# Softmax exponentials turned by a trip through DRAM and VectorE, in place of TensorE transposes

## The chip, the cores and the metric

The kernel runs on one core of one Trainium2 chip. The metric is device time in microseconds (us) of one execution of the whole program; lower is better. The kernel before has a median of 1646.08 us over three runs (1644.12 to 1647.88).

A core has five engines with a queue of instructions each, and each engine takes its own in order: TensorE (PE: matrix products, results to PSUM banks), VectorE (DVE), ScalarE (ACT), GpSimd (POOL) and SyncE (SP, which here only issues DMAs). PEld is the loading of TensorE's stationary operand. DMAs are issued from SP's queue and, a few, from ACT's.

## The reference, cut to what matters

One transformer block on x of 2048 tokens by 1024 channels, all in float32. There is one attention head of width 256.

```
qkv  = layernorm(x) @ Wqkv + bqkv            # 1024 -> 3 x 256
p    = softmax(q @ k.T / 16)                 # 2048 x 2048
attn = (p @ v) @ Wo + bo                     # 256 -> 1024
x1   = x + layernorm(attn)
h    = layernorm(x1)
y    = (silu(h @ Wg.T) * (h @ Wu.T)) @ Wd.T  # 1024 -> 2752 -> 1024
out  = x1 + layernorm(y)
```

## The kernel before, in words

**Precision.** TensorE multiplies in fp32r. Each float32 operand is split into a high part (an ACT copy that rounds) and a low part (VectorE: source minus high part), and a product is three matmuls: high by high, high by low, low by high (`mm3`, lines 126 to 130).

**Stages.** First q, k and v for all tokens (0 to about 140 us of the profiled span). Then attention over 16 blocks of 128 queries (`for i in range(NT)`, to about 410 us). Then the gated feed-forward in two halves of the tokens (the rest, lines 869, 1055 and 1056).

**One attention block i.** The loop body works on three blocks at once:

- `scores(i+1, j)`, j = 0 to 3: six matmuls of 512 columns into `bank[j]`, then a VectorE maximum of the bank (line 265).
- `softmax(i+1)`: two small VectorE operations make the bias (lines 440, 441), ACT takes four exponentials of 512 columns from the banks into `p_s` and sums them (line 443).
- `turn(i, j)`: four TensorE transposes of 128 by 128 from `p_s` into bank 4 or 7 (line 452), then ACT and VectorE split the bank into high and low parts of `pT` (lines 111, 112). It brings keys onto partitions.
- `attend(i)`: 16 pairs of matmuls into `bank[6]`, 512 columns with the high part of p (line 468) and 256 columns with the low part (line 469); ACT copies half of the bank to `o`, VectorE adds the other half (lines 470, 471).
- `turn_o(i-1)`: two TensorE transposes of `o` into `bank[5]` (line 478), split by ACT (480) and VectorE (481) into `oTs`.
- `proj(i-1)`: twelve matmuls of 512 columns of `oTs` by the output weights, into banks 5 and 7; VectorE scales by the softmax denominator and adds the bias (line 491).
- For the first eight blocks (`EARLY`), also: statistics of proj's result (`out_stats`), normalize and add x (`residual`), store x1, normalize again, store the result spread over partitions (`spread`, an ACT-issued DMA, line 597), load it back (`gather`, 600), turn it in 32 by 32 tiles on VectorE (`xpose`, 604), store it (606).

**What sets the order.** The code is given in program order to a planner that holds a cost for each instruction and lays down one fixed order for each engine. `pin` (`tc.keep_in_program_order`) keeps an instruction in the order of the code among others so marked; `tc.issue_after(x)` puts instructions behind x. On the chip each engine follows its fixed order and waits for operands. In the order laid down for the kernel before, TensorE has `turn_o(i-1)`, then `attend(i)`, with `proj(i-1)` and `scores(i+2)` mixed into the latter half, and the transposes of `turn` in groups of four all through the block.

Of the kernel before, what the change touches and what calls it, by code (L numbers as in the profile page):

```python
# [15 lines left out]
P = 128  # L16
# [18 lines left out]
def block_kernel(ctx, tc, x, xt, wqk, wqk_t, wv, bqk, bv, wo, bo, wgu, wlast, wd, out):  # L35
# [48 lines left out]
    x1_d = [tl(dram, [P, C], F32, f"x1_d{t}") for t in range(NT)]  # L84
    xn_d = [tl(dram, [P, C], F32, f"xn_d{t}") for t in range(NT)]
# [172 lines left out]
    def scores(i, j, pin=lambda i: i):  # L258

        cols = slice((i % TB) * P, (i % TB + 1) * P)  # L260
        q = qa if i < TB else qs[(i // TB) % 2]
        for d in range(2):
            k = kT(d, j)
            mm3(bank[j], (q[:, d, 0, cols], q[:, d, 1, cols]), (k[:, 0, :], k[:, 1, :]), d == 0, d == 1, pin)
        nc.vector.tensor_reduce(ys[i % 4][:, j : j + 1], bank[j], AX.X, ALU.max)
# [170 lines left out]

    def softmax(i):

        s = ys[i % 4]
        nc.vector.tensor_reduce(s[:, 4:5], s[:, 0:4], AX.X, ALU.max)  # L440
        nc.vector.tensor_scalar(s[:, 5:6], s[:, 4:5], -1.0 / 16.0, None, ALU.mult)
        for j in range(4):
            nc.scalar.activation(p_s[:, j * 512 : j * 512 + 512], bank[j], AF.Exp, bias=s[:, 5:6], scale=1.0 / 16.0, accum_out=s[:, 8 + j : 9 + j])
        nc.vector.tensor_reduce(s[:, 12:13], s[:, 8:12], AX.X, ALU.add)
        nc.vector.reciprocal(s[:, 13:14], s[:, 12:13])
# [10 lines left out]
    def attend(i):  # L456
# [10 lines left out]
        for k in range(NKB):  # L467
            nc.tensor.matmul(b, p[:, k, 0, :], vt(k).rearrange("p h d -> p (h d)"), start=(k == 0), stop=False)  # L468
            nc.tensor.matmul(b[:, D:], p[:, k, 1, :], vt(k, 0), start=False, stop=(k == NKB - 1))  # L469
# [5 lines left out]
    def turn_o(i, pin=lambda i: i):  # L475
# [4 lines left out]
        last_o[0] = nc.scalar.copy(oTs[i % 2][:, :, 0, :], b)  # L480
        last_o[1] = pin(nc.vector.tensor_tensor(oTs[i % 2][:, :, 1, :], b, f32(oTs[i % 2][:, :, 0, :]), ALU.subtract))
        return t

    def proj(i):
        a = pair[i % 3][0] if i < EARLY else f4[i % 2] if i < NT - 1 else xe
        oT = oTs[i % 2]
        for h, b in ((1, bank[5]), (0, bank[7])):
# [3 lines left out]
            nc.vector.scalar_tensor_tensor(a[:, cols], b, ys[i % 4][:, 13:14], bo_s[:, cols], ALU.mult, ALU.add)  # L491
# [3 lines left out]

    def out_stats(t, a):

        m, r, s = norm_stats([a[:, 0:512], a[:, 512:1024]], tc.keep_in_program_order if t >= EARLY else None)
        nc.gpsimd.tensor_scalar(s[:, 16:17], m, r, -1.0, ALU.mult, ALU.mult)
        return r, s  # L500

    def residual(t, a, xt, st=None, pin=lambda i: i):

        r, s = st or out_stats(t, a)
        pin(nc.scalar.activation(a, a, AF.Identity, bias=s[:, 16:17], scale=r))
        (nc.gpsimd if t >= EARLY else nc.vector).tensor_tensor(xt, xt, a, ALU.add)
# [82 lines left out]

    def wo_split(d):  # L590
        pin(nc.scalar.copy(wo_s[:, d, 0, :], wr[d]))
        pin(nc.vector.tensor_tensor(wo_s[:, d, 1, :], wr[d], f32(wo_s[:, d, 0, :]), ALU.subtract))


    def spread(t, a):

        nc.scalar.dma_start(xn_d[t].rearrange("(i s) (g c) -> i s g c", i=4, g=4).rearrange("i s g c -> (s g) i c"), a.rearrange("p (i c) -> p i c", i=4))
# [605 lines left out]
    room = [(f4[2], f4[3]), (wr[1], xe)]  # L1203
    sts = {}
    for i in range(NT):
# [5 lines left out]
        turn(i, 0)  # L1211
        turn(i, 1)
        if i == NT - 1:
            for f in order[:2]:
                f.use()
            for f, r in zip(order[4:6], f4[2:4]):
                f.load(r)
        if more:
            scores(i + 1, 0)
            scores(i + 1, 1)  # L1220
        turn(i, 2)
        turn(i, 3)
        if more:
            scores(i + 1, 2)
            scores(i + 1, 3)
# [175 lines left out]
```

## Time and profile before

| | |
|---|---|
| median of 3 runs | 1646.08 us (1644.12 to 1647.88) |
| the profiled execution, its own time | 1644.92 us |
| its span in the trace | 1643.1 us |
| PE busy | 1633.6 us (99%) |
| DVE busy | 1122.5 us (68%) |
| ACT busy | 718.2 us (44%) |
| granted TensorE clock, mean | 1.00 |

The span is the time from the first to the last record in the trace; 1.8 us of the execution lie around it. A busy PE is not PE at its peak, since matmuls are pipelined and each lasts longer than the distance to the next. Of use here are therefore the starts: a 512-column matmul follows its predecessor by about 0.23 us, while each record is 0.39 us long. The same holds on a smaller scale for VectorE and ACT, where an operation may start some 0.08 us ahead of the end of the one before it.

### The profile page before, as it was taken

How to read it: one execution, taken by the hardware profiler on the slowest of the kernel's cores; microseconds unless marked ns; L12 is line 12 of the kernel's file. 1: busy time of each engine (PE TensorE's matmuls, PEld its weight loads, DVE VectorE, ACT ScalarE, POOL GpSimd, SP SyncE). 2: the span in 40 equal slices, each digit the busy share in tenths (PEclk: the TensorE clock that was granted, in tenths of full speed). 3: DMA queues.
4: the chain of work that ended last, by engine and by line, in shares of the span. 5: the costliest groups of instructions: out<-in, count | busy, mean ns of one | idle time of the engine just before them, and what ended most of it. 6: DMA issues, size and time to landing. Idle time of an engine off the chain costs nothing.

```text
span 1643.1 us, 20860 instructions
## 1 busy us (share of the span) xinstructions
PE 1633.6 (99%) x7576; PEld 1361.1 (83%) x7576; DVE 1122.5 (68%) x1676; ACT 718.2 (44%) x1061; POOL 108.7 (7%) x157
## 2 busy tenths in 40 slices
PE   9999999999999999999999999999999999999998
PEld 8888888888888888888888888888888888888887
DVE  6656787778778888787577458855666655455458
ACT  5663445436444444433465344433333333354342
POOL 3120000000011111120000001100000000000001
PEclk9999999999999999999999999999999999999999
DMA  9452145556657777677477657532222333686663
GB/s 324 164 178 69 52 158 189 167 199 210 232 172 242 252 252 246 227 237 264 156 250 248 195 182 236 199 104 96 97 96 96 103 103 121 242 260 195 192 190 121
DMA packets 148184, 300.38 MB, mean 183 GB/s; under 512 B 14576, under 2 KB 39792, under 8 KB 148080
## 3 DMA queue, kind: packets, MB, share of 16 engines
q1 hardware_dynamic: 138480, 288.69, 53.1%
q10 hardware_dynamic: 9600, 10.36, 2.0%
q8 instruction: 59, 0.97, 0.2%
q14 instruction: 45, 0.37, 0.1%
HBM read 206.70 MB, written 92.29 MB: 182 GB/s over the span
## 4 chain that ended last, share of the span: by engine, by line
PE 94%; DVE 2%; DMA 2%; issue 1%; ACT 0%; POOL 0%; SPq 0%; POOLq 0%; DVEq 0%; ACTq 0%
PE bank L869 71%; PE bank L128 4%; PE bank L130 4%; PE bank L129 4%; PE bank L468 3%; PE bank L469 2%; PE bank L452 2%; PE bank L246 1%; PE bank L247 1%; PE bank L311 1%; DVE a L112 0%; DMA f<-xn_d 0%; DMA f<-wv 0%; DMA xn_d<-f 0%; PE bank L1056 0%
## 5 line engine op out<-in xcount | busy, mean ns | idle before, releaser
L869 PE MATMUL bank<-a 128*128 128x512 f32 (+1 forms) x960 | 226.4, 386 | 0.0
L869 PE MATMUL bank<-xb,a 128*128 128x512 f32 x912 | 212.5, 389 | 0.1
L869 PEld LDWEIGHTS bank<-a 128*128 128x128 f32 x960 | 179.1, 188 | 36.6
L869 PEld LDWEIGHTS bank<-xb,a 128*128 128x128 f32 x912 | 170.9, 188 | 35.8 <-DVE a L112 0.5
L111 ACT CAST a<-f2p 128x1024 fp32r<-128x1024 f32 (+2 forms) x123 | 106.9, 869 | 124.7 <-PE bank L869 89.5
L112 DVE TENSOR_TENSOR a<-f2p,a 128x1024 fp32r<-128x1024 f32 (+2 forms) x123 | 122.4, 995 | 44.1 <-ACT a L111 37.7
L869 PE MATMUL bank<-kx,a 128*128 128x512 f32 x612 | 145.2, 389 | 0.0
L869 PEld LDWEIGHTS bank<-kx,a 128*128 128x128 f32 x612 | 114.9, 188 | 23.8
L112 DVE TENSOR_TENSOR a<-f,a 128x1024 fp32r<-128x1024 f32 (+1 forms) x70 | 79.9, 1141 | 61.3 <-ACT a L111 59.0
L869 PE MATMUL bank<-wvo 128*128 128x512 f32 (+1 forms) x498 | 120.9, 387 | 0.0
L869 PEld LDWEIGHTS bank<-wvo 128*128 128x128 f32 x498 | 93.0, 188 | 18.9
L111 ACT CAST a<-f 128x1024 fp32r<-128x1024 f32 (+1 forms) x70 | 57.6, 823 | 101.1 <-PE bank L869 96.2
L869 PE MATMUL bank<-a,a 128*128 128x512 f32 x420 | 99.6, 389 | 0.3 <-ACT p_s L931 0.3
L869 PE MATMUL bank<-kx,wvo 128*128 128x512 f32 x420 | 99.3, 389 | 0.0
L883 DVE TENSOR_TENSOR xi<-bank,xi 128x512 f32<-128x512 f32 (+1 forms) x90 | 60.9, 681 | 48.5 <-PE bank L869 42.2
L869 PEld LDWEIGHTS bank<-a,a 128*128 128x128 f32 x420 | 78.8, 188 | 17.1 <-ACT p_s L931 0.8
L869 PEld LDWEIGHTS bank<-kx,wvo 128*128 128x128 f32 x420 | 78.8, 188 | 16.3
L112 DVE TENSOR_TENSOR wvo<-f,wvo 128x1024 fp32r<-128x1024 f32 (+1 forms) x47 | 54.6, 1162 | 53.1 <-ACT wvo L111 53.1
L869 PE MATMUL bank<-a1b,wvo 128*128 128x512 f32 x360 | 86.6, 389 | 0.0
L883 DVE TENSOR_TENSOR p_s<-bank,p_s 128x512 f32<-128x512 f32 x80 | 53.9, 681 | 46.7 <-PE bank L869 42.9
L869 PEld LDWEIGHTS bank<-a1b,wvo 128*128 128x128 f32 x360 | 67.6, 188 | 14.0
L869 PE MATMUL bank<-kx 128*128 128x512 f32 (+1 forms) x339 | 78.5, 387 | 0.0
(341 smaller groups left out, 3063.7 us busy)
## 6 DMA issues: line engine op xcount, KB each, us to landing
f2p<-wgu SPq DMA_DIRECT2D x41, 512.0 KB, 5.5
f<-x SPq DMA_DIRECT2D x28, 512.0 KB, 6.0
f<-wgu SPq DMA_DIRECT2D x22, 512.0 KB, 3.5
wr<-wgu SPq DMA_DIRECT2D x21, 512.0 KB, 4.9
hd_S<-xi SPq DMA_DIRECT2D x42, 256.0 KB, 4.4
f<-wd SPq DMA_DIRECT2D x20, 512.0 KB, 4.1
td_T<-f SPq DMA_DIRECT2D x40, 256.0 KB, 5.0
f2p<-td_T SPq DMA_DIRECT2D x40, 256.0 KB, 3.0
```

Of the source, the lines that this page charges most:

```text
L111: nc.scalar.copy(hi, src)
L112: (lo_engine or nc.vector).tensor_tensor(lo, src, f32(hi), ALU.subtract)
L128: pin(nc.tensor.matmul(o, w[0], m[0], start=first, stop=False))
L129: pin(nc.tensor.matmul(o, w[0], m[1], start=False, stop=False))
L130: return pin(nc.tensor.matmul(o, w[1], m[0], start=False, stop=last))
L246: pin(nc.tensor.matmul(b, xg[:, c, 0, cols], wv_s[:, c, :, :].rearrange("p a f -> p (a f)"), start=(c == 0), stop=False))
L247: pin(nc.tensor.matmul(b[:, D:], xg[:, c, 1, cols], wv_s[:, c, 0, :], start=False, stop=(c == 7)))
L452: nc.tensor.transpose(b[:, n * P : (n + 1) * P], p_s[:, k * P : (k + 1) * P], ident)
L468: nc.tensor.matmul(b, p[:, k, 0, :], vt(k).rearrange("p h d -> p (h d)"), start=(k == 0), stop=False)
L469: nc.tensor.matmul(b[:, D:], p[:, k, 1, :], vt(k, 0), start=False, stop=(k == NKB - 1))
L869: one = nc.tensor.matmul(o, w[i], m[j], start=first and n == 0, stop=last and n == 2, skip_group_check=chained)
L883: nc.vector.tensor_tensor(o, a, b, op)
```

## The change

For query blocks 2 to 12 (`SPREAD`) the TensorE transposes of p go away. ACT writes the exponentials into `p_s` in another order within a partition, and after each half (two banks) issues a DMA that stores 512 KB into `pt_d`, spread so that its 1 KB pieces change partitions (`by_quarter`). In the next block SP loads each half back (`collect`) into `wr[0]` and `wr[1]`, VectorE turns it there in 32 by 32 tiles (`turn_half`, 1024 columns), ACT takes the high part (`high_half`) and VectorE the low part (`low_half`), again 1024 columns each.

The queries of a block come out permuted, which `turn_o` undoes with a strided read of the bank. The steps of such a block are pinned on VectorE and ACT in the order of the code, and `attend(i)` is put behind `proj(i-1)` on TensorE, with its matmuls grouped by eight: eight of 512 columns, then eight of 256.

The early norms are computed otherwise. The rows of the output weights and the bias are centred (`minus_mean`, `wo_split`, `center_bo`: ACT sums, POOL scales, ACT subtracts), so that proj's result has mean zero and its scale needs only ACT's sum of squares (`out_stats`). The residual is one VectorE operation (a * r + x), and the second norm uses the mean of x and ACT's sum of squares. VectorE's four `bn_stats` of a block go; ACT gets two squares in place of one scaling. `first_sums` uses other tiles (`room`).

```diff
+    SPREAD = range(2, NT - 3)
+    def by_quarter(d):
+        return d.rearrange("(i s) (g c) -> i s g c", i=4, g=4).rearrange("i s g c -> (s g) i c")
+    def collect(i):
+        for h in range(2):
+            nc.sync.dma_start(wr[h], pt_d[i][h])
+    def turn_half(i, h):
+        pin(nc.vector.transpose(wr[h], wr[h]))
+    def high_half(i, h):
+        high, low, r = half_of(i, h)
+        pin(nc.scalar.copy(high, r))
+    def low_half(i, h):
+        high, low, r = half_of(i, h)
+        pin(nc.vector.tensor_tensor(low, r, f32(high), ALU.subtract))
...
+            pin(nc.scalar.activation(o, b, AF.Exp, bias=s[:, 5:6], scale=1.0 / 16.0, accum_out=s[:, 8 + j : 9 + j]))
+            if i in SPREAD and j % 2 == 1:
+                pin(nc.scalar.dma_start(by_quarter(pt_d[i][h]), p_s[:, h * C : h * C + C].rearrange("p (i c) -> p i c", i=4)))
...
-        for k in range(NKB):
-            nc.tensor.matmul(b, p[:, k, 0, :], vt(k).rearrange("p h d -> p (h d)"), start=(k == 0), stop=False)
-            nc.tensor.matmul(b[:, D:], p[:, k, 1, :], vt(k, 0), start=False, stop=(k == NKB - 1))
+        n = 8 if i in SPREAD else 1
+        for k0 in range(0, NKB, n):
+            for k in range(k0, k0 + n):
+                nc.tensor.matmul(b, p[:, k, 0, :], vt(k).rearrange("p h d -> p (h d)"), start=(k == 0), stop=False)
+            for k in range(k0, k0 + n):
+                nc.tensor.matmul(b[:, D:], p[:, k, 1, :], vt(k, 0), start=False, stop=(k == NKB - 1))
...
     def out_stats(t, a):
-        m, r, s = norm_stats([a[:, 0:512], a[:, 512:1024]], tc.keep_in_program_order if t >= EARLY else None)
-        nc.gpsimd.tensor_scalar(s[:, 16:17], m, r, -1.0, ALU.mult, ALU.mult)
-        return r, s
+        s = small_tile()
+        nc.scalar.activation(xe, a, AF.Square, accum_out=s[:, 0:1])
+        return scale_of(s)
+    def residual(t, a, xt, r, pin):
+        pin(nc.vector.scalar_tensor_tensor(xt, a, r, xt, ALU.mult, ALU.add))
+        nc.sync.dma_start(x1_d[t].rearrange("(g s) c -> s g c", g=4), xt)
+        s, m = small_tile(), m_of(t // TB, t % TB)
+        nc.gpsimd.tensor_scalar(s[:, 4:5], m, -1.0, None, ALU.mult)
+        nc.scalar.activation(a, xt, AF.Square, bias=s[:, 4:5], accum_out=s[:, 0:1])
+        r = scale_of(s)
+        nc.gpsimd.tensor_tensor(s[:, 5:6], s[:, 4:5], r, ALU.mult)
+        nc.scalar.activation(a, xt, AF.Identity, bias=s[:, 5:6], scale=r)
...
     for i in range(NT):
+        if i in SPREAD:
+            collect(i)
+            scores(i + 1, 0, hold=pin)
+            scores(i + 1, 1, hold=pin)
+            turn_half(i, 0)
+            high_half(i, 0)
+            scores(i + 1, 2, hold=pin)
+            scores(i + 1, 3, hold=pin)
+            largest(i + 1, pin)
+            turn_o(i - 1, hold=pin)
+            turn_half(i, 1)
+            exponentials(i + 1, (0, 1), pin)
+            high_half(i, 1)
+            exponentials(i + 1, (2, 3), pin)
+            low_half(i, 0)
+            projected = proj(i - 1, pin)
+            low_half(i, 1)
+            denominator(i + 1, pin)
...
+        if i in SPREAD:
+            with tc.issue_after(projected.ins):
+                attend(i)
```

The order that the planner lays down for the changed program, from block 4 on, is for TensorE: the last 13 of the 24 matmuls of `scores(i+1)` (banks 1 to 3), the two transposes of `turn_o(i-1)`, the twelve of `proj(i-1)` (two into bank 7, six into bank 5, four into bank 7), eight of `attend(i)` with 512 columns, eleven of `scores(i+2)` (banks 0 and 1), eight of 256, eight of 512 and eight of 256 columns, which ends `attend(i)`. For VectorE: the addition that ends `attend(i-1)`, the maxima of banks 0 and 1, `turn_half(i, 0)`, the maxima of banks 2 and 3, `largest`, the low part of `turn_o(i-1)`, `turn_half(i, 1)`, `low_half(i, 0)`, the two scalings of `proj(i-1)`, `low_half(i, 1)`, `denominator`, `residual(i-2)`, `xpose(i-3)`. For ACT: the copy that ends `attend(i-1)`, `high_half(i, 0)`, the high part of `turn_o(i-1)`, two exponentials, a DMA issue, `high_half(i, 1)`, two exponentials, a square, a DMA issue, a square, a scaling, a DMA issue.

## The prediction

> **What bounds the kernel now.** I read the page's busy table and its list of waits for TensorE first, to see which engine sets the time and whether it ever starves. Then the chain that ended last, for the length of one attention block, and the timeline of one block's end, for the steps that the change puts between products.
>
> ```profile
> PE 1633.6 (99%) x7576; PEld 1361.1 (83%) x7576; DVE 1122.5 (68%) x1676; ACT 718.2 (44%) x1061; POOL 108.7 (7%) x157
> ...
> PE bank L128 <- DVE oTs L481: 0.8, 2, 0.4
> ```
>
> TensorE is busy all through, and in the whole run it waits 0.8 us for `oTs`, the operand of `proj`. So only fewer or shorter TensorE steps gain, and any new wait of TensorE costs its full length.
>
> ```profile
> 263.36 0.44 PE bank L452 x4
> ...
> 343.01 0.44 PE bank L452 x4
> ...
> 273.73 0.27 PE L469 MATMUL bank<-a1b,a 128*128 128x256 f32 x1
> 273.84 0.40 PE L128 MATMUL bank<-wvo,oTs 128*128 128x512 f32 x1
> 274.04 0.37 ACT L470 COPY f<-bank 128x256 f32<-128x256 f32 x1 [1.03 <-PE bank L469]
> 274.45 0.42 DVE L471 TENSOR_TENSOR f<-bank,f 128x256 f32<-128x256 f32 x1
> ...
> 228.39 1.24 DVE L604 STREAM_TRANSPOSE f<-f 128x1024 f32<-128x1024 f32 x1
> 229.55 0.11 DVE L122 TENSOR_SCALAR small<-small 128x1 f32<-128x1 f32 x1
> 229.58 0.68 DVE L265 TENSOR_REDUCE ys<-bank 128x1 f32<-128x512 f32 x1
> 230.18 0.68 DVE L118 BATCH_NORM_STATS2 small<-f 128x6 f32<-128x512 f32 x1
> 230.77 0.68 DVE L265 TENSOR_REDUCE ys<-bank 128x1 f32<-128x512 f32 x1
> 231.36 0.41 DVE L481 TENSOR_TENSOR oTs<-bank,oTs 128x256 fp32r<-128x256 f32 x1
> ...
> 187.47 1.05 ACT L434 CAST qb<-f 128x1024 fp32r<-128x1024 f32 x1
> 188.41 1.25 ACT L505 ACTIVATE f<-f,small 128x1024 f32<-128x1024 f32 x1
> ...
> 288.00:304.00 16.00, 16.00 (x87) 13.42 (x86) 12.46 (x27) 8.05 (x16) 1.62 (x4) 1.00 0.69 229
> ```
>
> From the chain: one block lasts 15.93 us ((343.01 - 263.36)/5). From the timeline: `attend` ends at 273.84 (the next matmul's start); ACT's copy starts 0.20 later, VectorE's addition 0.61 later. VectorE starts a 512-column step every 0.60, a 32x32 turn is followed after 1.16, a 256-column step after 0.33; a hand-over between engines takes 0.04. The window shows DMA at 0.69 share for 229 GB/s, so about 332 GB/s at full share.
>
> **The parts.** *Removed.* Four groups of transposes in each of 11 blocks. In the timeline of 262 to 273 us they take 0.52, 0.44, 0.45 and 0.45 from the start of the group to normal pace again: 1.86 a block, 20.5 in all. If TensorE stayed fed, that would be the gain.
>
> *Moved: `proj(i-1)` straight behind `turn_o(i-1)` on TensorE.* Before, `attend` lay between and covered the split of `oTs`. Now TensorE has, after the end E of the last `attend`, 13 matmuls of 0.227 and two transposes (0.14): free at E+3.1. What it needs comes by VectorE's fixed order: copy and hand-over to E+0.61, addition to 0.94, two maxima to 2.14, `turn_half` 2.14 to 3.38 (L604; next start at 3.30), two maxima, the second with a dependent successor (0.68 + 0.04), to 4.62, `largest` 0.18 + 0.06, `turn_o`'s low part 4.86 to 5.27. ACT: `high_half` from 3.42 (1.05, next start after 0.94, lines 434 and 505), `turn_o`'s high part 4.36 to 4.73. So `proj`'s first two matmuls start at E+4.77 and end at 5.23, the other ten wait for the low part until 5.31: TensorE stands 1.67 + 0.08 = 1.75 us. Then ten matmuls 2.27, eight of 512 columns 1.82, eleven 2.50, and 8 of 256, 8 of 512, 8 of 256: 0.955 + 1.82 + 0.955 (256 columns in a row: 2.63 us for 22, line 464). The next E is E+15.63, against 15.93: -0.30 a block, **-3.3** in 11 blocks. A restart from a wait costs about 0.1 (a matmul behind transposes: 0.33 to its successor instead of 0.23): **+1.1**.
>
> *Block 2*, the first of the kind: VectorE's order has the scaling of `proj(0)`, whose matmuls are TensorE's last before `turn_o(1)`, ahead of the maxima. From the last matmul: 0.20 + 0.66 + 1.20 + 1.24, then `high_half` and the high part 0.04 + 0.94 + 0.37 + 0.04 = 4.7 against 0.14 for the transposes: 4.55 in place of 1.67, **+2.9**. *Block 12*: ahead of the maxima VectorE has a split of `first_sums` (1.14, behind 1.05 of ACT from E+0.57) and two sums (2 x 0.60), so the maxima begin at E+3.96, not 0.94; one more sum sits before `largest` (+0.48): about **+3.4**.
>
> *The loop over VectorE and ACT.* From one copy of `o` to the next where ACT has the last scaling and the spread's issue ahead of it (six blocks): addition to the low part of `turn_o` 4.64, its own 0.33, two turns and splits and two scalings of `proj` 1.15 + 1.15 + 2 x 0.66 + 1.15, denominator 0.26, residual 1.22, square with its sum 1.15 + 0.19 (line 207), three POOL steps about 1.5 (lines 123 and 499: 0.55 and 0.27 and gaps of 0.1), scaling 1.25, issue 0.4, hand-overs and the drain of dependent steps 0.3: 15.9, against 15.73 for TensorE's: **+0.9**.
>
> *DMA.* A block of the middle moves nine 512 KB transfers instead of five: 4.72 MB, 14.2 us at 332 GB/s. `pt_d`'s first half is issued at about E+6.4 (bias at 4.98, two exponentials at 0.67) and must be in `wr[0]` at E+15.63+2.14: 11.4 us. The same two shapes before, issue to landing, least, median and most: the spread store 2.9, 5.6, 8.2, the gather 3.2, 4.0, 6.1 (0.3 for SP's issue): 9.9 by medians, 14.6 by the worst. Gain is excluded, so the bounds are 0 and 9 blocks x 3.2 = 29. With DMA nearly full I let half of the transfers find one more ahead (0.8 each, two per trip), which uses up the slack; I take 0.2 a block: **+1.8**. The second half has as much time (due at 20.8, issued at 9.3 to 10.5), and a late second turn is first taken up by `low_half(0)`, due 4 us after its nominal end. Queues: behind a waiting `collect` on SP stand the stores of x1 and xT, x's load and the gather; `xpose` has 3.7 us of room before the next E, and x is needed two blocks on.
>
> *Strided read of the bank in `turn_o`* (steps of 32 elements). Nearest by operation: the same two steps now, 0.37 and 0.42. Nearest by stride: ACT's strided copy of 1024 (line 221) at 2.19 against 1.05, 1.1 ns more an element, 0.28 for 256, on ACT and VectorE in turn: 0.56 x 11 = 6.2. I take **0**, as the operand is PSUM and not SBUF as there, and keep 6.2 as the other end. The runs of 32 elements in `high_half`, `low_half` and the exponentials have the pattern of `xpose`, which at 1.24 is no slower than other turns or sums of 1024 (1.22): 0.
>
> "SBUF — State Buffer" of the Trainium skill (section on the DMA port swizzle, on cachelines) says that an access pays when it crosses to a new 16-byte line, and PSUM has lines of 8 bytes. Line 221 agrees. By that rule `turn_o`'s reads pay too, and my sum would be 6.2 higher; no row shows it for PSUM.
>
> *Edits that I cost at nothing.* Norms by squares: VectorE loses four statistics (0.60 each) a block; ACT gets two squares for one scaling, in the loop above; POOL's additions are in it too. Centring: ACT gets about 4.2 us in blocks 0 and 1, in its gap from 158.9 to 161.5 and later ones; the copies behind it slip 0.3 us, within the half block until their bank is needed; uncovered it would be 1. The weight loads into `f2p[1]` and `wr[0]` come a block later, with about 16 us still to their first use.
>
> **Sum**: -3.3 + 1.1 + 2.9 + 3.4 + 0.9 + 1.8 = +6.8. On the profiled execution's 1644.9 that is 1651.7; it lay 1.2 under the median of the runs, so I forecast 1653.
>
> "TensorE: Matmul & The Clock Gate" (Part 1) says that after an idle window of about 3.4 us the array runs at half clock for as long again. The trace grants 1.00 everywhere but never idles so long. By that rule the waits of blocks 2 and 12 (4.6 and 5.1 us) could cost up to 1.7 each, 3.4 more in all.
>
> **Rivals.** *(B) The DRAM trip sets the pace*: turns wait for `collect`. For it: DMA near full, and a worst pair of 14.6 against 11.4. Against: medians fit. At 1 to 3 us late in nine blocks, 1662 to 1680; the strided reads alone give 1659. *(C) The wait is shorter than I sum, not slower*: the turn in place is contiguous, and VectorE's one-input cast of 256 (line 334, 0.29) beats the two-input 0.42, a rate that makes 0.69 of 1.24. Then the wait shrinks by 0.5 a block, 6 in all: 1647; without the late DMAs 1645. From 0.35 a block on, the kernel is not slower. Against: line 604 is the same instruction at 1.24. *(D) TensorE stays fed*: all 20.5 gained, 1626. For it: only the claim that other products fill the gap. Against: TensorE takes its order as it is, and `proj` follows `turn_o` in it.
>
> **How the numbers follow.** Sum as forecast, 1649.5 to 1662: 0.47. B: 0.20. C: 0.23, of which half is below 1642.8 if VectorE's other steps are quicker too. D and mixtures with it: 0.10. 0.2% (3.3 us) is about what can be told from no change. Faster: 0.10 + 0.09 = 0.19; same: 0.14; slower: 0.67. Range 1640 to 1676: down to C with all special costs gone, up to B at 2.5 us a block; forecast's own range 1649 to 1662.
>
> **What would show.** PE's waits should list `proj`'s first lines behind ACT and VectorE's steps on `oTs`, 11 times, some 1.7 us each, 4 to 5 in blocks 2 and 12; the period should be 15.7 to 15.9; VectorE's turns should be 1.24 and mostly not wait for `wr`. I am wrong if these waits are under 1.3, or if turns wait on DMA.

## The result and the profile after

The changed kernel has a median of 1662.77 us over four runs (1660.81 to 1665.83), the kernel before 1645.63 us over four runs on the same chip. The ratio is 1.0105, with a 95% interval from 1.0084 to 1.0125: the change costs about 17 us, 1%. The profiled execution took 1661.64 us, its span is 1659.8 us, against 1643.1 us before.

The page of the changed kernel, busy time by engine:

```profile
PE 1623.7 (98%) x7400; PEld 1347.9 (81%) x7400; DVE 1118.0 (67%) x1612; ACT 730.6 (44%) x1070; POOL 116.6 (7%) x176
```

TensorE's list of waits from 139 to 427 us, the attention stage. Columns: what TensorE was about to do, whom it waited for, us in total, times, the longest.

```profile
PE bank L129 <- ACT oTs L530: 18.8, 10, 4.6
PE bank L129 <- DVE ys L465: 3.9, 1, 3.9
PE bank L515 <- DVE a L461: 2.0, 1, 2.0
PE bank L129 <- DVE oTs L531: 1.6, 1, 1.6
```

TensorE issues 176 matmuls fewer, but where it waited 0.8 us for `oTs` it now waits 24.3 us at line 129, the first lines of `proj`, and 2.0 us for a low part of p. That is more than the 20.5 us of transposes removed.

The timeline of an undisturbed block, between the end of `attend` and `proj` (block 6):

```profile
246.57 1.24 DVE L453 STREAM_TRANSPOSE wr<-wr 128x1024 f32<-128x1024 f32 x1
247.40 0.38 PE L524 MATMUL bank<-ident,f 128*128 128x128 f32 x2
247.73 1.25 DVE L266 TENSOR_REDUCE ys<-bank 128x1 f32<-128x512 f32 x2
247.84 1.04 ACT L457 CAST a<-wr 128x1024 fp32r<-128x1024 f32 x1 [2.84 <-DVE wr L453]
248.79 0.36 ACT L530 CAST oTs<-bank 128x256 fp32r<-128x256 f32 x1
249.20 0.50 PE L129 MATMUL bank<-wvo,oTs 128*128 128x512 f32 x1 [1.42 <-ACT oTs L530]
249.27 0.42 DVE L531 TENSOR_TENSOR oTs<-bank,oTs 128x256 fp32r<-128x256 f32 x1
```

This is the chain that the prediction wrote down: turn, high half, high part of `oTs`, `proj`, with TensorE standing 1.42 us after its two transposes. The block lasts 15.8 us. So the ordinary block is as foretold. (The 1.42 counts from the end of the transposes' record; from the start of the first transpose to `proj` it is 1.80 us.) To find the 17 us, I take the start of `turn_o`'s transposes in each block i as a clock hand, counted from that of block 1, and subtract the same of the kernel before. The table gives how far a kernel is behind (us), for the changed kernel and for the experiments told of below.

| at block | 2 | 3 | 4 | 5 | 6 | 7 | 8 | 9 | 10 | 11 | 12 | 13 |
|---|---|---|---|---|---|---|---|---|---|---|---|---|
| changed kernel | -1.7 | 2.8 | 2.0 | 1.9 | 1.1 | 1.1 | 4.3 | 3.5 | 3.4 | 6.8 | 8.3 | 16.9 |
| warm | -1.7 | 1.5 | 1.2 | 1.1 | 0.6 | 2.2 | 5.6 | 5.4 | 6.0 | 9.4 | 9.3 | 14.3 |
| early_trip | -1.7 | 3.0 | 2.3 | 2.1 | 1.3 | 1.2 | 1.1 | 0.2 | 0.4 | 3.8 | 7.8 | 14.3 |
| half_trip | -1.7 | 3.1 | 2.3 | 2.1 | 1.4 | 1.3 | 1.1 | 0.3 | 0.1 | 1.2 | 8.5 | 14.4 |
| half_warm | -1.7 | 1.5 | 1.2 | 1.1 | 0.3 | 0.2 | 0.0 | -0.2 | -0.4 | -0.4 | 7.5 | 12.5 |
| sums_after | -1.7 | 3.9 | 3.1 | 3.0 | 2.2 | 5.1 | 5.1 | 4.2 | 7.0 | 10.1 | 9.3 | 10.6 |
| sums_half | -1.7 | 4.0 | 3.2 | 3.1 | 2.3 | 2.2 | 2.1 | 1.2 | 1.0 | 2.9 | 2.1 | 6.5 |
| sums_warm | -1.7 | 1.5 | 1.2 | 1.0 | 0.2 | 2.3 | 5.6 | 5.5 | 6.3 | 9.7 | 9.6 | 13.8 |
| all_out | -1.7 | 1.5 | 1.2 | 1.1 | 0.2 | 0.2 | 0.0 | -0.2 | -0.5 | 0.6 | 0.5 | 4.8 |

Row one: block 2 loses what it loses once (the first two columns go together, since the place of `turn_o` in the block moves), blocks 3 to 6, 8 and 9 win back 2.7 us together, and blocks 7 (+3.2), 10 (+3.4), 11 (+1.5) and 12 (+8.7) lose 16.8. Between blocks 13 and 15 1.6 us come back; the stage behind took 0.8 us more, and block 1 began 0.55 us later: 16.7 in all. The loss is made of single events.

The chain that ended last, at block 7 (start, us, what):

```profile
244.23 7.63 DMA wr<-pt_d
...
251.89 0.04 DVE wr L453
...
256.87 1.30 DVE f L560
...
260.64 1.25 ACT f L567
...
262.32 0.38 ACT f L516
```

The load of the second half of the exponentials lands 7.63 us after its issue. Its turn starts late, and everything behind it on VectorE with it: low half, scalings, the residual (L560), then its square and scaling on ScalarE (L567), and only then ScalarE copies `o` (L516). `proj` waits 3.26 us instead of 1.42.

Block 10 is late for another reason. VectorE's turn of x (L682) writes over a tile from which an earlier `proj` is still being stored to `at_d`, and waits for that store. Everything behind it in the fixed order, the first turn of exponentials included, starts late, and `proj` waits 3.25 us:

```profile
311.74 1.25 DVE L682 STREAM_TRANSPOSE f<-f 128x1024 f32<-128x1024 f32 x1 [4.17 <-DMA at_d<-f]
```

The same view as for block 7, before blocks 11 and 12:

```profile
335.82 7.61 DMA xe<-xT_d
343.43 0.02 issue
343.45 0.04 DVE xe L718
...
350.59 5.36 DMA f<-xT_d
...
356.04 0.69 DVE f L718
356.73 0.08 DVE ys L465
356.81 0.02 issue
356.84 0.15 DVE ys L466
356.99 0.34 DVE oTs L531
357.33 0.04 issue
357.38 0.79 PE bank L129
```

L718 are the sums of `first_sums`. They stand in VectorE's fixed order ahead of proj's scaling (block 11) and ahead of `turn_o`'s low part (block 12), and wait there for loads. TensorE waits behind them: 2.05 us in block 11, and in block 12 4.62 us for the high part of `oTs`, which comes behind the work of the split and the sums, and 1.59 for the low part, which comes behind a load.

The first of these loads start late because of a queue. The turn of x that they need ended at 325.17, but its store into `xT_d` was issued 3.2 us later, since SyncE's queue stood at `collect` (L445), which waits for a store of exponentials. In the kernel before, that store went out as soon as the turn had ended, at 327.44. From the same chain:

```profile
322.63 5.25 DMA pt_d<-p_s
...
327.94 0.32 SPq L445
...
328.35 6.53 DMA xT_d<-f
```

And the last thing, windows of one us (PE busy, PEld, DVE, ACT, POOL, then the granted clock, DMA share, GB/s), after the waits of blocks 2 and 10:

```profile
184.00:185.00 1.00, 0.00 (x0) 0.00 (x0) 1.00 (x3) 0.96 (x2) 0.00 (x0) 0.98 0.00 0
185.00:186.00 1.00, 0.59 (x1) 0.50 (x2) 0.93 (x5) 0.76 (x3) 0.00 (x0) 0.50 0.03 8
188.00:189.00 1.00, 1.00 (x5) 0.78 (x5) 0.24 (x2) 1.00 (x2) 0.00 (x0) 0.81 0.99 338
...
317.00:318.00 1.00, 0.96 (x4) 0.68 (x5) 0.49 (x3) 0.78 (x3) 0.00 (x0) 1.00 1.00 392
318.00:319.00 1.00, 1.00 (x4) 0.77 (x3) 0.07 (x1) 0.67 (x3) 0.00 (x0) 0.54 0.89 336
321.00:322.00 1.00, 1.00 (x4) 0.79 (x4) 1.00 (x3) 1.00 (x4) 0.00 (x0) 0.75 0.22 76
```

The clock falls to 0.50 for 3.4 us, and matmuls of 512 columns start 0.43 us apart instead of 0.23. It happens four times, from 184.96, 266.88, 318.08 and 355.63 us, the last time for 6.8 us. In these stretches TensorE worked 3.0, 3.4, 3.4 and 5.2 us; half of it, 7.5 us by this estimate, is lost.

### The profile page after: what moved, and what is told of

It is laid out like the page before. It is cut to its first block, busy times and chain, and to the rows that moved or that the text cites. A ratio compares the mean times of both kernels' runs of the same rounds, so it can differ in the third digit from the quotient of the medians.

```text
span 1659.8 us, 20502 instructions
## 1 busy us (share of the span) xinstructions
PE 1623.7 (98%) x7400; PEld 1347.9 (81%) x7400; DVE 1118.0 (67%) x1612; ACT 730.6 (44%) x1070; POOL 116.6 (7%) x176
## 4 chain that ended last, share of the span: by engine, by line
PE 91%; DMA 4%; DVE 3%; ACT 1%; issue 1%; SPq 0%; POOL 0%; POOLq 0%; ACTq 0%; DVEq 0%
PE bank L947 72%; PE bank L129 4%; PE bank L130 4%; PE bank L131 3%; PE bank L513 2%; PE bank L247 1%; PE bank L515 1%; DMA pt_d<-p_s 1%; DMA wr<-pt_d 1%; PE bank L248 1%; DVE ys L266 1%; PE bank L312 1%; PE bank L495 1%; DVE wr L453 0%; DMA xe<-xT_d 0%
## 5 line engine op out<-in xcount | busy, mean ns | idle before, releaser
L947 PEld LDWEIGHTS bank<-a,a 128*128 128x128 f32 x420 | 78.7, 188 | 16.8 <-ACT xi L1009 0.4
```

The source lines that it names most:

```text
L947: one = nc.tensor.matmul(o, w[i], m[j], start=first and n == 0, stop=last and n == 2, skip_group_check=chained)
```

## Experiments

The open question was how the loss divides among the trips through DRAM, `first_sums` in VectorE's order, the half clock, and the other edits. Ratios are to runs of the kernel before on the same chip; the last digits of medians on different chips are not compared. The expectations of no_spread to half_warm, covered and covered_2_8 count late blocks one lower: their blocks 6 and 9 are 7 and 10 here.

**No block through DRAM** (no_spread): the norms, the centring and the rooms alone.

```diff
-    SPREAD = range(2, NT - 3)
+    SPREAD = range(0)
```

> No block goes through DRAM; the norms by squares, the centred output weights and the four rooms for first_sums stay. Theory (these edits cost nothing, all of the +17 us belongs to the blocks through DRAM): 1645 us, within 3 of before. Rival (ScalarE's two squares and GpSimd's steps, or the weights' centring, cost part of it): 1649 us or more.

Measured 1646.47 us, ratio 1.0005 (0.9996 to 1.0014). These edits cost nothing, as the prediction had it.

**Seven blocks of eleven** (spread_2_8).

```diff
-    SPREAD = range(2, NT - 3)
+    SPREAD = range(2, 9)
```

> Only blocks 2 to 8 go through DRAM, 7 of 11; blocks 9 to 12 turn on TensorE as before. Theory (an undisturbed block is 0.15 us shorter; the loss is single events: block 2's wait with its half clock, +2.2 + 1.6, one late turn with its half clock, 1.8 + 1.7, and the rest in blocks 9 to 12 beside the loads of first_sums): 1650 to 1653 us. Rival (the loss is spread evenly, 1.5 us a block): 1656 us.

Measured 1654.10 us, ratio 1.0054 (1.0037 to 1.0071). The median is between the theory's 1653 and the rival's 1656 and the interval takes in both, so the total decides nothing. The trace does: at block 9 it is 6.4 us behind (3.5 at block 3, then late turns in blocks 6 and 7) and from there stays between 5.7 and 6.4, in blocks that turn on TensorE. So blocks 11 and 12 lose nothing to `first_sums` where `proj` is not placed this way.

**Trips with a block to spare** (early_trip).

```diff
-            nc.sync.dma_start(wr[h], pt_d[i][h])
+            nc.sync.dma_start(wr[h], pt_d[max(i - 1, 2)][h])
```

> Block i collects the pieces that block i-1 stored (its output is not the reference's), so that no load has to wait for a store just made; every transfer, instruction and order stays. Theory (late turns in blocks 6 and 9 to 12 come from the trip through DRAM): the two waits of 3.3 us fall to 1.4, their half-clock stretches go with them, 1654 to 1657 us. Rival (bandwidth and SyncE's queue make them late whatever the trip): 1661 to 1664 us.

Measured 1658.98 us, ratio 1.0082 (1.0067 to 1.0097). Block 7's late turn is gone (1.1 behind at block 8, 4.3 in the changed kernel). Block 10 stays late (+3.4): there the chain goes over the store of `at_d` that VectorE's turn of x (L682) waits for, 5.40 us here. The total lies between the theory's 1657 and the rival's 1661. The theory was right for block 7 and not for block 10, and blocks 11 and 12 lost 10.5 us all the same.

**TensorE kept at work in the waits** (warm).

```diff
+            for _ in range({2: 36, 12: 40}.get(i, 12)):
+                warm = pin(nc.tensor.transpose(bank[4][:, 0:P], ident, ident))
+            with tc.issue_after(warm.ins):
-            projected = proj(i - 1, pin)
+                projected = proj(i - 1, pin)
```

> 12 transposes of the identity into an unused bank stand ahead of proj in each block through DRAM, 36 in block 2 and 40 in block 12 (0.11 us each), in time in which TensorE waited. Theory (long waits are followed by 3.4 us and more at half clock, 7.6 us in all): the waits' ends stay where they are, the granted clock stays at 1.00, 1654 to 1657 us. Rival (the clock costs little, or falls for another reason): 1661 to 1664 us, with half-clock stretches as before.

Measured 1661.51 us, ratio 1.0097 (1.0082 to 1.0112): the total is the rival's. But in block 2 the clock now stays at 1.00. The windows of warm there:

```profile
183.00:184.00 1.00, 1.00 (x11) 1.00 (x10) 1.00 (x2) 0.45 (x1) 0.28 (x1) 1.00 0.00 0
186.00:187.00 1.00, 1.00 (x6) 0.80 (x5) 1.00 (x2) 0.56 (x3) 0.00 (x0) 1.00 0.00 0
```

`proj` starts 4.35 us after `turn_o`, exactly as without the transposes, so the wait is the same; yet at block 3 the kernel is 1.5 us behind and not 2.8. Half clock in block 2 costs 1.3 us. The gain did not last: blocks 6, 7 and 10 lost 1.6, 3.4 and 3.4 us, and at block 11 warm was 9.4 us behind against 6.8. In blocks 7 and 10 TensorE still waited 1.95 and 1.94 us behind the twelve transposes, and the clock fell there. A TensorE that comes sooner may find the transfers later; with one trace of each kernel that is not shown.

**Half the bytes of each trip** (half_trip).

```diff
-            nc.sync.dma_start(wr[h], pt_d[i][h])
+            nc.sync.dma_start(wr[h][0:64], pt_d[i][h][0:64])
...
-                pin(nc.scalar.dma_start(by_quarter(pt_d[i][h]), p_s[:, h * C : h * C + C].rearrange("p (i c) -> p i c", i=4)))
+                pin(nc.scalar.dma_start(by_quarter(pt_d[i][h])[:, 0:2], p_s[:, h * C : h * C + C].rearrange("p (i c) -> p i c", i=4)[:, 0:2]))
```

> Each store of exponentials and each load of them moves 64 of 128 rows, 256 KB for 512 KB (the other half of the turned tile is old data, so the output is not the reference's); instructions, orders and waits stay. A block of the middle moves 3.67 MB instead of 4.72. Theory (the DMA engines' load, 0.9 to 1.0 of their time in blocks 3 to 12, makes the trips late, and late trips make the waits of 3 us and more in blocks 6 and 9 to 12): waits of 1.4 there, block 2's and block 12's own delays stay, 1649 to 1654 us. Rival (the pinned orders and SyncE's queue make those waits, whatever the load): 1659 to 1663 us.

Measured 1659.98 us, ratio 1.0069 (1.0042 to 1.0096). The windows from 187 to 315 us, of the kernel before, of the changed kernel and of half_trip:

```profile
187.00:315.00 128.00, 127.56 (x687) 107.45 (x687) 102.56 (x207) 66.60 (x130) 12.19 (x30) 1.00 0.53 173
```

```profile
187.00:315.00 128.00, 116.51 (x558) 95.27 (x556) 94.80 (x141) 71.74 (x132) 18.39 (x42) 0.98 0.89 292
```

```profile
187.00:315.00 128.00, 116.92 (x566) 95.85 (x565) 98.23 (x147) 74.03 (x137) 17.86 (x42) 0.99 0.75 238
```

The change takes the DMA engines' share from 0.53 to 0.89; with half the trips' bytes it is 0.75, and block 7 is in time, block 10 nearly: 1.2 us behind at block 11 for 6.8. Up to there the theory holds. Then the gain is lost: blocks 11 and 12 take 13.2 us more than before, and the total is the rival's. VectorE's timeline in block 11 of half_trip says why:

```profile
326.53 0.65 DVE L266 TENSOR_REDUCE ys<-bank 128x1 f32<-128x512 f32 x1
330.69 0.69 DVE L718 TENSOR_TENSOR f<-f 128x512 f32<-128x512 f32 x1 [3.51 <-DMA f<-xT_d]
331.30 0.68 DVE L266 TENSOR_REDUCE ys<-bank 128x1 f32<-128x512 f32 x1
331.99 0.69 DVE L718 TENSOR_TENSOR xe<-xe 128x512 f32<-128x512 f32 x1
...
333.93 0.41 DVE L531 TENSOR_TENSOR oTs<-bank,oTs 128x256 fp32r<-128x256 f32 x1
```

Between the maxima of banks 2 and 3 stands a sum of `first_sums` that waits 3.51 us for its load, and three more stand ahead of `turn_o`'s low part. TensorE, two matmuls into `proj`, waited 5.66 us. With half the bytes this wait is still there. The data come from the last turn of x, one block before, which ended at 319.54; its store was issued at 321.43, again behind a `collect` that waited in SyncE's queue.

half_trip changes two things at once, the load of the DMA engines and the length of a trip itself (its loads landed after 3.7 us in the median where whole ones took 5.2). Transfers that kept their 512 KB landed sooner too: of the six spread stores from `f` between 187 and 363 us the median is 3.8 us before, 7.3 in the changed kernel and 6.1 here. So the load has a part in it; how the two divide is not shown.

**Both together** (half_warm).

```diff
+            nc.sync.dma_start(wr[h][0:64], pt_d[i][h][0:64])
...
+            for _ in range({2: 36, 12: 40}.get(i, 12)):
+                warm = pin(nc.tensor.transpose(bank[4][:, 0:P], ident, ident))
```

> half_trip and warm together: with little lateness left, the transposes of the identity keep TensorE at work in the waits of blocks 2 and 12 and in all others. Theory (half clock after a long wait costs 1.5 to 2 us each time): 3 to 4 us under half_trip, clock at 1.00. Rival (the clock's part is small): within 1 us of half_trip.

Measured 1663.04 us, ratio 1.0093 (1.0071 to 1.0115), above half_trip, so in the total both guesses missed. In attention it is 1.9 us ahead of half_trip (12.5 against 14.4 at block 13), and up to block 11 it is 0.4 us *ahead* of the kernel before. But the time from block 15 to the end was 1262.7 us, against 1255.8 in half_trip. In the profiles of this study that stage took between 1253.5 us (before) and 1262.7 us; no_spread has 1257.2. In half_warm TensorE waits 6.9 us of it for ScalarE's line 1009, in half_trip 0.9; what makes ScalarE late there I have not found. From here on the table decides, not the totals.

**first_sums behind the denominator** (sums_after).

```diff
             denominator(i + 1, pin)
+            cb = i - EARLY - 3
+            if cb >= 0:
+                first_sums(cb, *room[cb], pin)
...
-        if 0 <= cb < 4:
+        if 0 <= cb < 4 and i not in SPREAD:
             first_sums(cb, *room[cb])
```

> One thing is changed: in blocks 11 and 12 first_sums (its split and its four sums, which wait for loads of xT_d) stands behind the block's denominator on VectorE, not between the maxima and turn_o's low part; blocks are counted by i. Theory (these sums and the loads they wait for hold VectorE's pinned order, and through oTs TensorE: blocks 11 and 12 took 41.9 us for two, 31.5 undisturbed): 8 to 10 us less than the changed kernel, 1652 to 1656 us. Rival (the DMA engines are full there, and the loss comes back as later trips): 1660 us or more.

Measured 1660.02 us, ratio 1.0071 (1.0053 to 1.0088). Blocks 11 and 12 now lose 0.5 us together (10.1 to 10.6 in the table) where the changed kernel loses 10.2. That much is the place of `first_sums`. The total fell by less than the theory's 8 to 10 us and lies at the rival's 1660, because in this execution blocks 6, 9 and 10 lost 2.9, 2.8 and 3.1 us, where the changed kernel lost 3.2 and 3.4 in blocks 7 and 10, though the order of the instructions up to there is the same: which transfers are late, and when, varies from one execution to the next.

**The same with half the bytes** (sums_half).

```diff
+            nc.sync.dma_start(wr[h][0:64], pt_d[i][h][0:64])
...
             denominator(i + 1, pin)
+            cb = i - EARLY - 3
+            if cb >= 0:
+                first_sums(cb, *room[cb], pin)
```

> sums_after and half_trip together. Theory (what is left of the loss is the late trips of blocks 7 and 10, which half_trip takes away): only block 2's wait with its half clock stays against 0.15 us a block, 0.999 to 1.002 of before. Rival: 1.004 of before or more.

Measured 1653.48 us, ratio 1.0032 (1.0019 to 1.0045). Block 2's loss (4.0 here) stays, and block 12 lost 4.4 us: a sum of block 13 that was not pinned had floated ahead of block 12's scalings. The ratio lies between the two guesses.

**All three causes out** (all_out): half the bytes, TensorE kept at work, and every sum pinned.

```diff
+            nc.sync.dma_start(wr[h][0:64], pt_d[i][h][0:64])
...
+            for _ in range({2: 36, 12: 40}.get(i, 12)):
+                warm = pin(nc.tensor.transpose(bank[4][:, 0:P], ident, ident))
...
-        if 0 <= cb < 4:
-            first_sums(cb, *room[cb])
+        if 0 <= cb < 4 and i not in SPREAD:
+            first_sums(cb, *room[cb], pin)
```

> half_trip, warm and sums_after together, with the sums of blocks 13 and 14 pinned at their place too (one of them floated into block 12 in sums_half). Theory (late trips from the DMA engines' load, VectorE's pinned order with first_sums in it, and half clock after waits are the whole loss): from turn_o of block 1 to that of block 13 between 190 and 193 us, against 191.6 before the change and 208.5 with it; in all 0.998 to 1.003 of before, since the stage behind attention differs by 0 to 6 us between kernels. Rival (something else costs as well): more than 196 us for that stretch.

Measured 1654.71 us, ratio 1.0041 (1.0027 to 1.0054). From block 1 to block 13 it took 196.4 us, 0.4 over the rival's bound. Of these, 2.7 are my own: in block 12 the wait had shrunk to 1.4 us (sums_after), but 40 transposes of 0.11 stood in it, so `proj` came 4.50 us after `turn_o` instead of 1.80. Up to block 12 it is 0.5 us behind, without them 2.1 at block 13. TensorE's only wait from 187 to 363 us is in block 10, where the turn of x still waited 2.00 us for the store of `at_d`:

```profile
PE bank L129 <- ACT oTs L530: 1.3, 1, 1.3
```

So the three causes explain the loss in attention, 16.9 us, to within about 2 us. The rest of the ratio is the last stage, which took 1260.4 us here.

**The bytes alone** (sums_warm): all_out with whole trips, stores and loads. Against all_out:

```diff
-            nc.sync.dma_start(wr[h][0:64], pt_d[i][h][0:64])
+            nc.sync.dma_start(wr[h], pt_d[i][h])
...
```

> all_out with whole trips: 512 KB a transfer again. Theory (the DMA engines' load alone then makes late trips): 4 to 9 us more than all_out from turn_o of block 1 to that of block 13, 195 to 202 us, all of it in blocks 5 to 12. Rival (with the sums in their place and TensorE at full clock the trips are in time): 190 to 194 us.

Measured 1661.14 us, ratio 1.0071 (1.0053 to 1.0089). From block 1 to 13 it took 205.4 us, 9.0 more than all_out, the whole of it in blocks 6, 7, 9 and 10, as the theory had it, though the stretch as a whole lies over its 202. VectorE's waits between 187 and 363 us show the turns waiting for trips, which in all_out they do not:

```profile
DVE wr L453 <- DMA wr<-pt_d: 7.2, 4, 3.2
```

**An order with proj covered** (covered, covered_2_8). `attend` is split in two halves and six score matmuls are kept for after `turn_o`'s transposes.

```diff
+            m = [scores(i + 1, j, hold=pin) for j in range(2)][1]
+            if i - 1 in SPREAD:
+                with tc.issue_after(m.ins):
+                    m = attend_part(i - 1, 8, 16)
+                attend_out(i - 1, pin)
+            with tc.issue_after(m.ins):
+                m = scores(i + 1, 2, hold=pin)
+            with tc.issue_after(m.ins):
+                m = turn_o(i - 1, hold=pin)
+            turn_half(i, 0)
+            high_half(i, 0)
+            with tc.issue_after(m.ins):
+                m = scores(i + 1, 3, hold=pin)
...
+            with tc.issue_after(m.ins):
+                projected = proj(i - 1, pin)
```

> TensorE's order written out: scores of banks 0 and 1, second half of attend, scores of bank 2, turn_o's transposes, scores of bank 3, proj, first half of attend; the two maxima of banks 0 and 1 stand ahead of o's addition on VectorE, turn_half behind turn_o's low part. Theory (proj waits because the split of oTs stands behind maxima and a turn, with nothing left for TensorE to do): the wait falls from 1.42 to under 0.4 us a block, and the DMA engines set the pace, 4.72 MB at 332 GB/s or 14.2 us against 15.8 a block where all goes well: 1636 to 1650 us. Rival (the DMA engines already set the pace, and what TensorE gains comes back as later trips): 1657 to 1663 us.

> The order of covered in blocks 2 to 8 alone, 9 to 12 as before the change. Theory: without the blocks that share the DMA engines and VectorE with first_sums, 1636 to 1643 us, faster than before. Rival (as for covered): 1650 to 1654 us, as spread_2_8.

Measured 1.0041 (1.0025 to 1.0058) and 1.0017 (1.0002 to 1.0032), 1654.22 and 1649.64 us. covered lies between the theory's 1650 and the rival's 1657, covered_2_8 at the rival's end. TensorE does not wait at `proj` from block 3 on, and an undisturbed block takes 14.0 to 14.1 us. Other waits took the place: in covered 2.1, 3.4, 1.6 and 4.9 us ahead of `turn_o`, for `o`, and 2.8 in block 2 for the split of q. The chains of these four differ. Two go back over the residual and the split of q to a turn that waited for its trip; one over ScalarE's copy of `o` and the residual to a scaling of `proj` that waits for a store of `xT_d`; the longest to the turn of x that waits for the store of `at_d`.

**Two moves more** (covered2_2_8, covered2): the residual ahead of proj's scalings, and the split of q in block 2 earlier; covered2 also has `first_sums` as in sums_after.

```diff
+            if i == 2:
+                q_split(1, pin)
             exponentials(i + 1, (2, 3), pin)
+            if i < EARLY + 2:
+                residual(i - 2, *pair[(i - 2) % 3], sts[i - 2], pin)
+                spread(i - 2, pair[(i - 2) % 3][0])
```

> covered_2_8 with two moves: the residual of block i-2 and its spread stand ahead of proj's scalings, so that ScalarE has done them when attend ends, and q's split in block 2 stands ahead of the exponentials of banks 2 and 3. Theory (the waits of 1.9 to 3 us for o's addition in covered_2_8 are ScalarE's copy of o standing behind the residual): they go, 0.993 to 0.998 of before. Rival (the DMA engines set the pace, so that turns become late in their place): 1.000 of before or more.

> The orders of covered2_2_8 and of sums_after in blocks 2 to 12. Theory (TensorE's wait at proj, the residual ahead of o's copy and first_sums ahead of turn_o's low part are the whole loss): 0.990 to 0.998 of before. Rival (nine transfers of 512 KB a block at 332 GB/s, 14.2 us, and their lateness keep the period near 15.5): 1.000 of before or more.

Measured 1.0055 (1.0037 to 1.0074) and 1.0066 (1.0047 to 1.0085), 1656.86 and 1658.72 us: worse than covered, and what the rivals had, though not by their mechanism alone. In covered2 `o` came late by 5.0, 5.0 and 5.5 us, in blocks 4, 8 and 9.

**The same with half the bytes** (covered_half), against covered2:

```diff
-            nc.sync.dma_start(wr[h], pt_d[i][h])
+            nc.sync.dma_start(wr[h][0:64], pt_d[i][h][0:64])
```

> covered2 with half of each trip's bytes and all sums pinned. Theory (the order of covered2 lets a block run in 14.8 us, seen in its undisturbed blocks, and the DMA engines' load alone takes this back): 177 to 184 us from turn_o of block 1 to that of block 13, 0.990 to 0.997 of before. Rival (VectorE's order, not the load, makes its waits of 5 us): over 190 us for that stretch, 1.000 of before or more.

Measured 1655.02 us, ratio 1.0044 (1.0028 to 1.0060); the stretch from block 1 to 13 took 191.6 us, so the rival was right: with half the load the waits stayed (4.9, 2.8 and 3.8 us). The chains lead to the split of q, which in blocks 4 and 8 stood on ScalarE behind the residual (in block 4 the chain starts at a load of exponentials that took 7.53 us at half the bytes), and to the turn of x in block 9, which overwrites a tile that proj of block 8 is still storing.

**These places mended** (covered3, covered3_2_10), with whole trips.

```diff
-        a = pair[i % 3][0] if i < EARLY else f4[i % 2] if i < NT - 1 else xe
+        a = pair[i % 3][0] if i <= EARLY else f4[i % 2] if i < NT - 1 else xe
...
             exponentials(i + 1, (2, 3), pin)
+            if i % TB == 0 and TB <= i < NT - TB:
+                q_split(i // TB + 1, pin)
```

> covered2 with whole trips and three places mended: q's split in blocks 4 and 8 stands behind the exponentials and ahead of the residual, proj of block 8 writes a tile that the turn of x's block 6 does not overwrite, and all sums are pinned. Theory (three of covered2's waits of 5 us, in blocks 4, 8 and 9, are these places, and each brought a half-clock stretch): 15 to 20 us less than covered2 over blocks 2 to 12, 0.994 to 0.999 of before. Rival (the DMA engines' load makes other waits in their place): 1.002 of before or more.

> The same for blocks 2 to 10 alone, before first_sums begins. Theory: as covered3, within 3 us of it. Rival (the step back to transposes on TensorE costs 5 us, as in covered2_2_8): 4 us or more over covered3.

Measured 1.0038 (1.0024 to 1.0051) and 1.0032 (1.0015 to 1.0049), 1654.70 and 1654.13 us: the rival for covered3, the theory for covered3_2_10. At block 13 covered3 is 4.0 us behind, covered2 was 12.8: half of the forecast gain. The splits of q were still badly placed, two waits of 4.4 and 4.7 us in blocks 4 and 8.

**And q's splits once more** (covered4).

```diff
             with tc.issue_after(m.ins):
                 m = turn_o(i - 1, hold=pin)
+            late_q = i % TB == 1 and TB < i < NT - TB
+            if late_q:
+                q_high(i // TB + 1)
             turn_half(i, 0)
...
+            if late_q:
+                q_low(i // TB + 1)
             with tc.issue_after(m.ins):
                 projected = proj(i - 1, pin)
```

> covered3 with the splits of q's second and third groups in blocks 5 and 9, ScalarE's part behind turn_o's high part and VectorE's behind the residual; in covered3 they stood in blocks 4 and 8 ahead of the block's own splits, which were 4.4 and 4.7 us late there. Theory (these two places, with a half-clock stretch after each, are what is left of covered3's loss): 10 to 13 us less than covered3, 0.994 to 0.998 of before. Rival (turns late by the DMA engines' load take their place): 1.000 of before or more.

Measured 1649.28 us over 12 runs, ratio 1.0011 (1.0002 to 1.0020): the rival. In the profiled execution, one of the faster of the twelve, no wait in attention is over 2.0 us, the clock stays up, and from block 1 to 13 it is 0.6 us behind the kernel before. TensorE's waits from 187 to 363 us are many and small:

```profile
PE bank L527 <- DVE a L469: 9.2, 9, 2.0
PE bank L540 <- DVE f L533: 4.0, 8, 1.3
PE bank L525 <- ACT a L465: 1.4, 2, 1.0
```

The larger ones go back to turns that wait for a trip, as in this line of VectorE's timeline:

```profile
234.99 1.25 DVE L461 STREAM_TRANSPOSE wr<-wr 128x1024 f32<-128x1024 f32 x1 [5.24 <-DMA wr<-pt_d]
```

Ten turns waited 1.2 to 5.2 us for their trips. What the covered order wins, the trips take. No version of this study beats the kernel before.

## Why the prediction was right in direction and short in size

It said +7 us, and 17 were measured. By its own steps:

- **Right: proj's wait replaces the transposes.** The sum let `proj` start 0.14 + 1.67 = 1.81 us after the first transpose of `turn_o`; in blocks 4 to 6 and 9 it started 1.80 after. Blocks 4 to 6 took 15.77 to 15.80 us where the sum had 15.63 and 0.1 for the restart, so against 15.93 a block wins 0.14 and not 0.2. (The 2.7 us of the table come mostly from blocks 3 and 8, which follow late ones, and block 5, which took 16.56 us before.) The rivals that had the wait shorter (C) or gone (D) were wrong; the turn took 1.24, as in the row it was taken from. All eleven waits at line 129 are there, but both signs of being wrong showed as well: in blocks 3, 8 and 11 they were 0.79, 0.46 and 0.74 us, under 1.3, and three turns waited for their trips.
- **Right: the edits costed at nothing**, shown by no_spread. The strided read of the bank, with 6.2 us as its other end, also costs nothing: line 530 took 0.36 and line 531 0.42 us, as 0.37 and 0.42 before. The rule of "SBUF — State Buffer" on 16-byte lines, carried over to PSUM's lines of 8 bytes at the price of line 221, would have put it at 6.2; no run here bears it out for PSUM.
- **Wrong, at no great cost: "The loop over VectorE and ACT".** Its listed terms add up to 16.0 us and not 15.9, and yet blocks 4 to 6 took 15.8: the +0.9 did not come.
- **Right in sum, wrong in make-up: block 2.** The sum had +2.7 in all, with `proj` 4.69 us after `turn_o`. It came 4.35 after (warm, without half clock, lost 1.5 us there), and half clock added the 1.3 that makes +2.8. That the totals agree is luck.
- **Wrong: "Block 12 ... about +3.4".** This is the step that failed most. It priced the split and the sums ahead of the maxima by their busy time, and that much came: `proj` of block 12 started 5.00 us after `turn_o`, 3.2 later than in an ordinary block. But it did not ask what they wait for. They wait for loads of `xT_d`, and in a pinned order a wait holds all that stands behind. Sums waited 4.69 and 0.92 us for loads in block 11, for which there was no term, and 1.23 in block 12; TensorE waited 2.05 us for it in block 11 and another 1.59 in block 12, and 2.6 of half clock followed. Blocks 11 and 12 cost 10.2 us; sums_after, which moves only these instructions, brought that to 0.5. The prediction named SyncE's queue, where stores wait behind `collect`, and gave it no price; 3.2 us of the 4.69 are that.
- **Wrong: DMA, "I take 0.2 a block: +1.8".** The mechanism was named and its bounds (0 to 29) held it, but the value was mis-sized. Blocks 7 and 10 cost 6.6 in the changed kernel, half clock included; whole trips in place of half ones cost 9.0 between all_out and sums_warm. The trips are not each a little late. Their medians, as the page of the changed kernel gives them, are below what was assumed, 4.1 + 4.9 us for 5.6 + 4.0 + 0.3:

```profile
pt_d<-p_s ACTq DMA_DIRECT2D x22, 512.0 KB, 4.1
wr<-pt_d SPq DMA_DIRECT2D x22, 512.0 KB, 4.9
```

But the slowest store took 9.89 us and the slowest load 7.63, and three turns of 22 waited, 0.70, 2.19 and 1.41 us. One of them, 2.19, made block 7 late. And "a late second turn is first taken up by `low_half(0)`" was wrong: block 7's chain passes through the residual to ScalarE's copy of `o`. That loop over VectorE and ScalarE had been summed at 15.9, a block's own length, so there was little slack to take up anything. Rival B was the mechanism of block 7. Block 10 was not a trip: "`xpose` has 3.7 us of room" failed there, when the turn of x waited 4.17 us for the store of `at_d`. No run changes this wait alone; it is there in early_trip, in half_trip (3.45) and in all_out (2.00).
- **Left out: the half clock.** The prediction cited "TensorE: Matmul & The Clock Gate" (Part 1) and kept 3.4 us out of the sum, because no row showed it. The trace shows four such stretches and 7.5 us. It is not a term of its own but makes each late event some 1.5 to 1.7 us dearer by that estimate, 2.6 after block 12.

What would have shown it beforehand: for each instruction ahead of a new wait in a pinned queue, the row of what *it* waits for, not only its duration.

## What to carry to other kernels

When work leaves the bound engine for a fixed order on another, that order becomes a chain, and a transfer that any instruction in it waits for can become a wait of the bound engine; price each by when it lands, not by the busy time of the instruction. Ask also what stands behind a waiting load in the queue that issues it. Here the median trip landed as assumed with the DMA engines 0.89 busy; a few slow ones made the loss. And where a loop over helpers is about as long as the block itself, lateness in it arrives nearly whole (block 7: a turn 2.19 us late, `proj` 1.89).

## What the runs showed of the hardware

**The clock falls on a grid.** The four falls of the changed kernel lie 81.92, 133.12 and 170.66 us after the first: 24.00, 39.00 and 50.00 times 3.413 us. In the fourteen other traces with two falls or more (the one at the program's end left out) these lie whole multiples of 3.413 us apart too, to 0.01 of a step (in covered3 19 and 34 steps after the first, in sums_after 20 and 39). "TensorE: Matmul & The Clock Gate" (Part 1) gives a free-running window of 3413 ns, and the traces agree. They differ in the rule: the page says half clock comes after an idle window, but no window had to be wholly idle. Laid on that grid, the windows at full clock in which TensorE's records leave 1.94 us or more empty were all followed by half clock (40 between 150 and 1600 us in all traces), those with 1.63 or less never. In between it went either way: 1.71 (all_out), 1.79 (sums_half) and 1.89 (covered_2_8) were, 1.82 (covered2_2_8) and 1.90 (half_warm) were not. So the limit is near half of a window. A wait of 2.95 us that the grid cut in two (covered_2_8, 1.59 and 1.36) passed, and one of 1.89 in one window did not.

**Transposes of the identity count as work for the clock**: 36 of them in 4.09 us kept it at 1.00 in block 2 of warm, where the wait without them was 3.91 and the clock fell. It did not fall there in half_warm, sums_warm and all_out either, which have the same transposes.
